# The first QKV stage of a conditioned transformer block: condition's rows first, the other small rows behind the modulation, filler transposes, weights in column slices

## The chip, the cores and the metric

The kernel runs on one core of a Trainium2 chip. The time is the device time of one execution in microseconds (us), and runs are compared by their medians. The engines are TensorE (PE; its weight loads are listed as PEld), VectorE (DVE), ScalarE (ACT), GpSimd (POOL) and SyncE (SP, which here only issues DMA transfers). Each engine works through its own instruction queue strictly in order; engines wait for each other and for transfers through semaphores.

## The reference

One transformer block whose two layer norms and two residual branches are modulated by a condition vector (batch 2, 2048 tokens, width 512, 16 heads, hidden width 2048):

```python
mod = silu(condition) @ Wada + bada
sh_a, sc_a, gt_a, sh_m, sc_m, gt_m = split(mod, 6, axis=1)
xn = layernorm(x, g1, be1)
xm = xn * (1.0 + sc_a[:, None, :]) + sh_a[:, None, :]
x = x + gt_a[:, None, :] * attention(xm, Wqkv, Wproj, bproj)   # causal
xn = layernorm(x, g2, be2)
xm = xn * (1.0 + sc_m[:, None, :]) + sh_m[:, None, :]
h = gelu(xm @ W1 + b1)
x = x + gt_m[:, None, :] * (h @ W2 + b2)
```

## The kernel before

The kernel goes through the two batch rows one after the other (a QKV stage, attention, projection each) and then through the MLP. The change lies in the first QKV stage, which also has to start everything: it loads the first tokens, the condition and the weights. In this stage 2048 tokens go by in groups of 512 (four tiles of 128 tokens), and for each group the queries, keys and values are made in blocks of 128 columns, most of them by a scheme with seven products in place of eight (`SUMS`: four extra weight blocks are sums and differences of the four that are loaded, `weight_sum`, on POOL). The very first block of queries and keys is made in the plain way (`plain`, tile `ps_qk`), so that it needs no sums.

What has to happen ahead of the first product:

- *Tokens.* `load_x(0)` (L919, SP) brings four tiles `x` of 256 KB. `stats` makes mean and variance (VectorE, L218 and L221); `inv_std` makes `rstd` (ScalarE Sqrt, L224; VectorE, L225 and L226); `scaled` applies them (ScalarE, L964, in place, one instruction for each tile). `norm(0, 0, ...)` transposes tiles 0 and 1 on TensorE (L214, tile `ps_xt`), `norm(0, 1, ...)` tiles 2 and 3.
- *Small rows.* The condition and the vectors g1, be1, g2, be2, b1, b2 are loaded as 44 rows of 128 numbers into one tile `rows` by seven DMAs that ScalarE issues (L1373). One transpose on TensorE (`ps_c`) and one copy on VectorE (L1402) turn them into columns, `cols`.
- *Modulation.* `load_wada(0, 1)` (L1391, SP) loads two 512 x 512 blocks of `Wada` in eight pieces of 256 KB into a free part of `vv`; POOL clears `mr` and loads `bada` into it. ScalarE makes `sc` = silu of the condition's columns (L1455). `modulation(0)` multiplies (tile `ps_mod`, eight products, shown as sixteen); `columns()` adds `bada` (VectorE, L1425), turns the result (`ps_modt`) and copies it to `mod`; `scale_shift` makes `a1` and `c1` out of it and of `cols`. `modulate` writes the modulated tokens `xmT` from the transposed ones (VectorE L269 and ScalarE L274).
- *Weights.* `load_w` (L926, SP) loads the four blocks of `Wqkv` for queries and keys, 512 KB each, `load_wv` (L936) the four for values. Behind them stand the sums on POOL (L944) and the tokens of the next group (L919 again).

ScalarE's functions come in tables. A function that is not in the loaded table needs an ACT_TABLE_LOAD ahead of it; the compiler puts it there. Silu and Sqrt lie in different tables. At L136 a tiny activation named `first` loads the Sqrt table early.

*What sets the order.* A scheduler of the framework orders each engine's instructions. What goes through `act()`, `mm()` or `transpose()` keeps the order in which it is written; the rest may move. Transfers that SP and ScalarE issue count their completions on eight semaphores, which are given out in turn over both queues, in the order in which the scheduler places the DMAs. A DMA that takes a semaphore first waits, on the engine that issues it, for the DMA that had the semaphore before it, which may be one of the other engine. In this kernel's built order the first eight are: `rows` (condition), x0, `rows` (g1), x1, `rows` (be1), `rows` (g2), x2, `rows` (be2). Then come x3, b1, b2, the eight pieces of Wada, `wqk` and `wv`.

The lines on which the waits of this case turn:

```python
def act(ins):
    return tc.keep_in_program_order(ins)

ps_c = ps_mm.tile([P, n_rows], F32, tag="mm", name="ps_c")
transpose(ps_c, rows)
nc.vector.tensor_copy(cols[:, :n_rows], ps_c)
```

Of the kernel before, what the change touches and what calls it, by code (L numbers as in the profile page):

```python
# [8 lines left out]
F32 = mybir.dt.float32  # L9
F32R = mybir.dt.float32r  # L10
BF16 = mybir.dt.bfloat16
AF = mybir.ActivationFunctionType
# [5 lines left out]
P = 128  # L18
# [9 lines left out]
def dit_block_kernel(  # L28
# [36 lines left out]
    nc = tc.nc  # L65
    B, T, D = x.shape
    HID = W1.shape[1]
    C = D // P
# [23 lines left out]
    ident = const.tile([P, P], F32, tag="ident", name="ident")  # L92
# [7 lines left out]
    eps = const.tile([P, 1], F32, tag="eps", name="eps")  # L100
# [16 lines left out]
    for n in range(2):  # L117

        f = bp.tile([P, QB + P], BF16, tag=f"fold{n}", name=f"fold{n}")
# [13 lines left out]


    first = const.tile([P, 1], F32, tag="first", name="first")
    nc.scalar.activation(first, eps, AF.Sqrt)  # L136


    cols = const.tile([P, 64], F32, tag="cols", name="cols")
# [15 lines left out]
    n_cond = B * C  # L155
    r_g1 = n_cond
    r_be1, r_g2, r_be2 = r_g1 + C, r_g1 + 2 * C, r_g1 + 3 * C
    r_b1 = r_g1 + 4 * C
    r_b2 = r_b1 + FC
    n_rows = r_b2 + C  # L160
# [36 lines left out]
    def col(r, n):  # L197
        return cols[:, r : r + n]
# [9 lines left out]
    def act(ins):  # L208

        return tc.keep_in_program_order(ins)  # L210

    def transpose(dst, src):
        n = src.shape[0]
        return tc.keep_in_program_order(nc.tensor.transpose(dst, src, ident[:n, :n]))  # L214
# [78 lines left out]
    ps_sp = ps_s_cm.__enter__()  # L293
# [590 lines left out]
    w_v = Wqkv.rearrange("(c p) f -> p c f", p=P)  # L884
# [11 lines left out]
    HK = C // 2  # L896

    class Qkv:
# [21 lines left out]
                xts.append(xt)  # L920
            self.xts[g] = xts

        def load_w(self, queue):
            for n, i, k in BASE:
                act(
                    queue.dma_start(  # L926
                        self.w[:, n], w_v[:, k * HK : (k + 1) * HK, i * D : (i + 1) * D]
                    )
                )

# [429 lines left out]
    with pool("wada") as wp, pool("qkv0") as qp, pool("hl0") as hp, pool(  # L1360
        "ps_qkv0", bufs=6, space=PSUM
    ) as ps_mm:
        rows = wp.tile([n_rows, P], F32, tag="rows", name="rows")
        for r, n, src in (
            (0, n_cond, cond.rearrange("b (c p) -> (b c) p", p=P)),
            (r_g1, C, g1.rearrange("(c p) -> c p", p=P)),
            (r_be1, C, be1.rearrange("(c p) -> c p", p=P)),
            (r_g2, C, g2.rearrange("(c p) -> c p", p=P)),
            (r_be2, C, be2.rearrange("(c p) -> c p", p=P)),
            (r_b1, FC, b1.rearrange("(c p) -> c p", p=P)),  # L1370
            (r_b2, C, b2.rearrange("(c p) -> c p", p=P)),
        ):
            nc.scalar.dma_start(rows[r : r + n, :], src)  # L1373
        wada_v = Wada.rearrange("(c p) f -> p c f", p=P)
        wada = {}

# [17 lines left out]
        qkv = Qkv(row, qp, ps_mm)  # L1394
        qkv.load_x(0)
        load_wada(0, 1)
        qkv.load_w(nc.sync)
        qkv.load_wv(hp, nc.sync)

        ps_c = ps_mm.tile([P, n_rows], F32, tag="mm", name="ps_c")  # L1400
        transpose(ps_c, rows)
        nc.vector.tensor_copy(cols[:, :n_rows], ps_c)  # L1402
        sc = wp.tile([P, C, HD], F32, tag="sc", name="sc")
        nc.vector.memset(sc, 0.0)

# [34 lines left out]
        def scale_shift(a, c, r_g, r_be, shift, scale):  # L1440
# [6 lines left out]
                )  # L1447
            nc.vector.tensor_tensor(c, c, mod[:, shift], ALU.add)

        for t in range(MTT):  # L1450
            qkv.stats(0, t)
        halves = [qkv.norm(0, 0, True)]

        act(
            nc.scalar.activation(  # L1455
                sc[:, :, :B], col(0, n_cond).rearrange("p (b c) -> p c b", c=C), AF.Silu
            )
        )
        picks()
        columns = modulation(0)  # L1460
        halves.append(qkv.norm(0, 1, True))
        columns()
        scale_shift(a1, c1, r_g1, r_be1, 0, 1)
        for k in range(0, C, 2):
# [62 lines left out]
    with pool("qkv1") as qp, pool("ps_qkv1", bufs=6, space=PSUM) as ps_mm:  # L1527
        qkv = Qkv(row, qp, ps_mm)
# [62 lines left out]
    with ExitStack() as mlp:  # L1591
        wp = mlp.enter_context(pool("mlpw", side="right"))
        ps_mm = mlp.enter_context(pool("ps2", bufs=4, space=PSUM))
# [733 lines left out]
```

## Time and profile before

| what | us |
| --- | --- |
| median of 3 runs | 2258.35 |
| the three runs | 2256.87, 2258.35, 2260.15 |
| the profiled execution | 2256.73 |
| its span, from the first to the last instruction | 2255.0 |
| mean granted TensorE clock, as a share of full speed | 0.997 |

A row of a timeline gives the start and the duration in us, the engine, the line of the kernel, the operation, output<-inputs by the program's names, their shapes, the count of instructions that were merged into the row, and in brackets how long the engine had been idle before and what ended that. ACTq and SPq are instructions that only issue a DMA. Rows of `ps_mod`, `ps_modt`, `ps_qk` and other float32 products show two entries for each product of the program. A row of a table of stretches gives for each engine its busy time and the count of instructions, and at its end the granted TensorE clock, the mean busy share of the sixteen DMA engines and the rate in GB/s.

### The profile page before, as it was taken

The page shows a single profiled execution, that of the slowest core. Times are in us where ns is not written, and L with a number is a line of the kernel's source. Part 1 is how long each engine was busy: PE and PEld are TensorE (multiplying, and loading weights), DVE is VectorE, ACT ScalarE, POOL GpSimd, SP SyncE. Part 2 cuts the span into 40 slices and gives each one's busy share as a digit, 9 for nine tenths or more (in the row PEclk, how much of TensorE's full clock was granted, in tenths as well). Part 3 has the DMA queues.
Part 4 walks back from the last instruction along what each step waited for, and adds up shares of the span by engine and source line. Part 5 has one row for each costly group of instructions (what it writes and reads, how often), then busy time and mean ns, then how long its engine had stood idle before and what let it go on. Part 6 is the DMA issues. An engine that isn't in the chain of part 4 may idle for free.

```text
span 2255.0 us, 33464 instructions
## 1 busy us (share of the span) xinstructions
PE 2211.3 (98%) x12057; PEld 1432.2 (64%) x12057; DVE 1535.7 (68%) x3309; ACT 1004.6 (45%) x2012; POOL 1297.9 (58%) x807
## 2 busy tenths in 40 slices
PE   7999999999999999999999999999999999999998
PEld 6777555555543587855555555345787787688687
DVE  4668766777757666777577767663685586576576
ACT  4434555555564244365656555614322422332410
POOL 4253998998983695199989898444205204304210
PEclk9999999999999999999999999999999999999999
DMA  8877143231324799542324113363353354353433
GB/s 281 251 259 193 43 93 75 62 85 48 106 97 135 252 308 313 142 92 62 85 67 104 44 48 131 109 231 129 109 175 133 123 184 145 108 187 126 158 125 110
DMA packets 160510, 311.57 MB, mean 138 GB/s; under 512 B 16544, under 2 KB 48844, under 8 KB 158552
## 3 DMA queue, kind: packets, MB, share of 16 engines
q1 hardware_dynamic: 155488, 285.53, 41.8%
q0 software_dynamic: 4480, 23.36, 2.7%
q8 instruction: 95, 1.56, 0.3%
q14 instruction: 71, 0.58, 0.1%
q10 hardware_dynamic: 376, 0.55, 0.1%
HBM read 229.95 MB, written 87.29 MB: 141 GB/s over the span
## 4 chain that ended last, share of the span: by engine, by line
PE 89%; DVE 4%; DMA 2%; POOL 2%; ACT 1%; issue 1%; SPq 0%; DVEq 0%; ACTq 0%; POOLq 0%
PE ps_a L206 27%; PE st L206 18%; PE ps_b L206 12%; PE o L206 10%; PE s L206 9%; PE ps_c L206 4%; PE ps_o L206 4%; PE sm L206 3%; DVE junk L498 1%; POOL ee L695 1%; PE ps_xt L214 1%; DMA x<-in_x_dram 1%; ACT e L670 1%; DVE mx L504 1%; PE ps_o L214 1%
## 5 line engine op out<-in xcount | busy, mean ns | idle before, releaser
L670 ACT ACTIVATE e<-st 128x512 f32<-128x512 f32 (+1 forms) x1152 | 575.0, 579 | 362.4 <-PE st L206 321.3
L504 DVE TENSOR_REDUCE mx<-s 128x1 f32<-128x512 f32 x576 | 381.9, 686 | 199.0 <-PE s L206 197.9
L695 POOL TENSOR_TENSOR ee<-ee,e 128x2048 f32<-128x2048 f32 x106 | 485.8, 4583 | 10.3 <-ACT e L670 4.3
L206 PE MATMUL st<-qst,kst 128*128 128x512 f32 (+3 forms) x1280 | 408.7, 386 | 0.0
L206 PE MATMUL s<-kst,qst 128*128 128x512 f32 (+3 forms) x1046 | 382.2, 396 | 8.0 <-DVE mx L498 2.7
L206 PE MATMUL ps_a<-sum,w 128*128 128x256 f32 (+1 forms) x1088 | 328.8, 431 | 0.1
L206 PE MATMUL o<-e,vv 128*32 128x512 f32 (+3 forms) x2560 | 293.2, 537 | 0.3 <-POOL e L682 0.3
L206 PEld LDWEIGHTS st<-qst,kst 128*128 128x128 f32 x1280 | 228.5, 188 | 97.3 <-issue 65.7
L498 DVE CUSTOM_DVE_ANT_0 junk<-s,causal 128x128 bf16<-128x128 f32 (+3 forms) x470 | 220.7, 470 | 61.0 <-PE s L206 46.8
L1795 POOL TENSOR_TENSOR sum<-w 128x256 f32<-128x256 f32 x30 | 21.8, 727 | 397.1 <-DMA w<-w1d 203.1
L206 PEld LDWEIGHTS s<-kst,qst 128*128 128x128 f32 x1046 | 195.4, 189 | 72.4 <-DVE mx L504 15.4
L206 PEld LDWEIGHTS ps_a<-sum,w 128*128 128x128 f32 x1088 | 204.5, 190 | 40.1 <-issue 11.4
L695 POOL TENSOR_TENSOR ee<-e 128x2048 f32<-128x2048 f32 x42 | 192.5, 4583 | 43.5 <-ACT e L670 42.5
L206 PEld LDWEIGHTS <-sel 32*128 32x128 bf16 x1152 | 29.5, 91 | 197.0 <-issue 196.1
L2014 ACT ACTIVATE h<-h,cols 128x512 f32<-128x512 f32 x120 | 76.8, 710 | 136.3 <-DVE h L1716 136.3
L504 DVE TENSOR_REDUCE mx<-st 128x1 f32<-128x512 f32 x192 | 131.0, 682 | 0.5
L682 POOL TENSOR_SCALAR_AFFINE_SELECT e<-e 128x512 f32<-128x512 f32 x128 | 83.3, 669 | 67.2 <-ACT e L670 67.2
L206 PE MATMUL st<-fold,sel 32*128 32x512 bf16 (+1 forms) x1152 | 117.3, 372 | 1.2
L206 PEld LDWEIGHTS o<-e,vv 128*32 128x32 f32 x2560 | 59.1, 108 | 92.3 <-issue 72.8
L1716 DVE TENSOR_TENSOR h<-c,ps_b 128x256 f32<-128x256 f32 x90 | 37.9, 421 | 103.5 <-PE ps_b L206 103.0
L1066 POOL TENSOR_TENSOR lo<-lo,hi 128x512 fp32r<-128x512 f32 x32 | 40.7, 1274 | 114.2 <-ACT hi L1064 109.8
L206 PE MATMUL ps_b<-sum,w 128*128 128x256 f32 (+1 forms) x384 | 95.0, 383 | 0.0
(237 smaller groups left out, 3590.7 us busy)
## 6 DMA issues: line engine op xcount, KB each, us to landing
qst<-q SPq DMA_DIRECT2D x128, 256.0 KB
kst<-k SPq DMA_DIRECT2D x128, 256.0 KB
w<-w1d SPq DMA_DIRECT2D x32, 896.0 KB
w<-w2d SPq DMA_DIRECT2D x28, 1024.0 KB
w<-w2d SPq DMA_DIRECT2D x28, 768.0 KB
q<-hi SPq DMA_DIRECT2D x32, 256.0 KB
q<-lo SPq DMA_DIRECT2D x32, 256.0 KB
k<-hi SPq DMA_DIRECT2D x32, 256.0 KB
```

The source lines that it names most:

```text
L206: return tc.keep_in_program_order(nc.tensor.matmul(*args, **kw))
L214: return tc.keep_in_program_order(nc.tensor.transpose(dst, src, ident[:n, :n]))
L498: nc.vector.tensor_tensor_reduce(junk[:, :w], x, causal[:, QB - w :], 1.0, MASKED, ALU.add, ALU.max, m,)
L504: self.vector(nc.vector.tensor_reduce(m, x, axis=AX.X, op=ALU.max))
L670: act(nc.scalar.activation(e4[:, h, :w], sts[h][:, :w], AF.Exp))
L682: nc.gpsimd.affine_select(d, d, pattern=[[0, HC], [1, P]], compare_op=ALU.is_ge, fill=0.0, base=0, channel_multiplier=-1,)
L695: act(nc.gpsimd.tensor_tensor(dst, x, y, ALU.add))
L1066: engine.tensor_tensor(lo, d, hi.bitcast(F32), ALU.subtract)
L1716: act(nc.vector.tensor_tensor(dst, x, y, ALU.add))
L1795: act(engine.tensor_tensor(dst, u, v, op))
L2014: nc.scalar.activation(d[j], d[j], AF.Gelu, bias=col(r_b1 + half * HF + fs[j], 1))
```

## The change

Six things change, all in the first QKV stage.

1. The condition's eight rows are loaded twice: first into a tile of their own, `rows_c`, then into `rows` as before. `rows_c` gets a transpose of its own, `ps_1`, and Silu reads that.
2. The small loads on ScalarE's queue go through `act()`, so their order is kept, and the Silu table is loaded by a tiny activation behind be1's load, ahead of the loads of g2, be2, b1 and b2.
3. Silu (`sc`) and a tiny Sqrt stand ahead of the statistics and the first `norm`; before, Sqrt was loaded first and Silu stood between the two halves of the tokens.
4. The transpose of `rows` and the copy to `cols` stand behind the second half's transposes, ahead of `columns()`.
5. TensorE makes 6 transposes of `ident` into a spare tile `ps_w` ahead of `ps_1` and 30 behind it.
6. The blocks of `Wqkv` for queries and keys are loaded in column slices: 128 columns of all four blocks, the next 128, then the last 256; twelve DMAs in place of four.

In the built order of the changed kernel the semaphores are given out to `rows_c`, x0, `rows` (condition), x1, g1, be1, x2, x3, then Wada 0 to 7, then g2, the first `wqk` piece, be2, the second piece, b1, the third, b2, the fourth, and the rest of `wqk`, `wv` and the next tokens. On POOL the memset of the next `mr`, which waits for `ps_modt`, and the two DMAs behind it stand among the weight sums instead of ahead of them.

```diff
--- before.py
+++ after.py
@@ -133,7 +133,6 @@
 
 
     first = const.tile([P, 1], F32, tag="first", name="first")
-    nc.scalar.activation(first, eps, AF.Sqrt)
 
 
     cols = const.tile([P, 64], F32, tag="cols", name="cols")
@@ -920,11 +919,12 @@
                 xts.append(xt)
             self.xts[g] = xts
 
-        def load_w(self, queue):
+        def load_w(self, queue, f=slice(0, D)):
             for n, i, k in BASE:
                 act(
                     queue.dma_start(
-                        self.w[:, n], w_v[:, k * HK : (k + 1) * HK, i * D : (i + 1) * D]
+                        self.w[:, n, :, f],
+                        w_v[:, k * HK : (k + 1) * HK, i * D + f.start : i * D + f.stop],
                     )
                 )
 
@@ -1361,6 +1361,7 @@
         "ps_qkv0", bufs=6, space=PSUM
     ) as ps_mm:
         rows = wp.tile([n_rows, P], F32, tag="rows", name="rows")
+        rows_c = wp.tile([n_cond, P], F32, tag="rowsc", name="rowsc")
         for r, n, src in (
             (0, n_cond, cond.rearrange("b (c p) -> (b c) p", p=P)),
             (r_g1, C, g1.rearrange("(c p) -> c p", p=P)),
@@ -1370,7 +1371,11 @@
             (r_b1, FC, b1.rearrange("(c p) -> c p", p=P)),
             (r_b2, C, b2.rearrange("(c p) -> c p", p=P)),
         ):
-            nc.scalar.dma_start(rows[r : r + n, :], src)
+            if not r:
+                act(nc.scalar.dma_start(rows_c, src))
+            act(nc.scalar.dma_start(rows[r : r + n, :], src))
+            if r == r_be1:
+                act(nc.scalar.activation(first, eps, AF.Silu))
         wada_v = Wada.rearrange("(c p) f -> p c f", p=P)
         wada = {}
 
@@ -1394,12 +1399,19 @@
         qkv = Qkv(row, qp, ps_mm)
         qkv.load_x(0)
         load_wada(0, 1)
-        qkv.load_w(nc.sync)
+        for f0, f1 in ((0, 1), (1, 2), (2, C)):
+            qkv.load_w(nc.sync, slice(f0 * P, f1 * P))
         qkv.load_wv(hp, nc.sync)
 
-        ps_c = ps_mm.tile([P, n_rows], F32, tag="mm", name="ps_c")
-        transpose(ps_c, rows)
-        nc.vector.tensor_copy(cols[:, :n_rows], ps_c)
+        ps_w = ps_sp.tile([P, P], F32, tag="s", name="ps_w")
+
+        def busy(n):
+            for _ in range(n):
+                transpose(ps_w, ident)
+
+        busy(6)
+        ps_1 = ps_sp.tile([P, n_cond], F32, tag="s", name="ps_1")
+        transpose(ps_1, rows_c)
         sc = wp.tile([P, C, HD], F32, tag="sc", name="sc")
         nc.vector.memset(sc, 0.0)
 
@@ -1447,18 +1459,23 @@
                 )
             nc.vector.tensor_tensor(c, c, mod[:, shift], ALU.add)
 
+        act(
+            nc.scalar.activation(
+                sc[:, :, :B], ps_1.rearrange("p (b c) -> p c b", c=C), AF.Silu
+            )
+        )
+        act(nc.scalar.activation(first, eps, AF.Sqrt))
+        busy(30)
         for t in range(MTT):
             qkv.stats(0, t)
         halves = [qkv.norm(0, 0, True)]
 
-        act(
-            nc.scalar.activation(
-                sc[:, :, :B], col(0, n_cond).rearrange("p (b c) -> p c b", c=C), AF.Silu
-            )
-        )
         picks()
         columns = modulation(0)
         halves.append(qkv.norm(0, 1, True))
+        ps_c = ps_mm.tile([P, n_rows], F32, tag="mm", name="ps_c")
+        transpose(ps_c, rows)
+        nc.vector.tensor_copy(cols[:, :n_rows], ps_c)
         columns()
         scale_shift(a1, c1, r_g1, r_be1, 0, 1)
         for k in range(0, C, 2):
```

## The prediction

> **What bounds the kernel now.** I read the page first, then the order of time on each engine over the first 30 us, because all of the change lies there.
>
> ```profile
> span 2255.0 us, 33464 instructions
> PE 2211.3 (98%) x12057; PEld 1432.2 (64%) x12057; DVE 1535.7 (68%) x3309; ACT 1004.6 (45%) x2012; POOL 1297.9 (58%) x807
> ```
>
> TensorE sets the end; whatever delays its first real product delays everything behind it. TensorE in order of time (start, duration, instruction, idle before and its releaser):
>
> ```profile
> 7.39 0.30 PE L214 MATMUL ps_c<-ident,rows 44*128 44x44 f32 x1 [7.39 <-DMA rows<-in_L_cond_b_dram]
> 9.19 0.48 PE L214 MATMUL ps_xt<-ident,x 128*128 128x128 f32 x1 [1.50 <-ACT x L964]
> 9.89 1.76 PE L214 MATMUL ps_xt<-ident,x 128*128 128x128 f32 x7 [0.23 <-ACT x L964]
> 11.58 2.75 PE L206 MATMUL ps_mod<-vv,sc 128*32 128x512 f32 x16
> 14.26 1.09 PE L214 MATMUL ps_xt<-ident,x 128*128 128x128 f32 x8
> 15.29 1.05 PE L206 MATMUL ps_modt<-pickc,mr 128*128 128x4 f32 x8
> 18.12 7.13 PE L206 MATMUL ps_qk<-xmT,wqk 128*128 128x512 f32 x16 [1.78 <-DVE xmT L269]
> ...
> 25.95 1.03 PE L206 MATMUL ps_b<-t,wqk 128*128 128x256 f32 x4
> 27.86 1.10 PE L206 MATMUL ps_a<-t,wqk 128*128 128x256 f32 x4 [0.89 <-POOL wqk L944]
> ```
>
> The first product is `ps_qk` at 18.12; from there TensorE hardly stops. Before it stands one chain: ScalarE scales the tokens `x`, TensorE transposes the first half, makes the modulation `ps_mod`, transposes the second half, and the modulated tokens `xmT` follow. ScalarE over the same stretch:
>
> ```profile
> 0.81 0.58 ACTq L1373 DMA_DIRECT2D rows<-in_cond_dram  x1
> ...
> 2.40 0.32 ACTq L1373 DMA_DIRECT2D rows<-in_L_cond_be_dram  x1
> 3.60 0.69 ACTq L1373 DMA_DIRECT2D rows<-in_L_cond_b_dram  x2
> ...
> 7.42 0.30 ACT L224 ACTIVATE rstd<-mv,eps 128x4 f32<-128x4 f32 x1 [1.61 <-DVE mv L221]
> 8.32 1.52 ACT L964 ACTIVATE x<-x,shift,rstd 128x512 f32<-128x512 f32 x2 [0.60 <-DVE shift L226]
> 9.86 1.28 ACT L1455 ACT_TABLE_LOAD   x1
> 11.15 0.21 ACT L1455 ACTIVATE sc<-cols 128x8 f32<-128x8 f32 x1
> ```
>
> The row to look at is 3.60. The fifth DMA issue ended at 2.72 and the sixth only began at 3.60. VectorE got its first tokens at the same moment:
>
> ```profile
> 3.60 0.69 DVE L218 BATCH_NORM_STATS2 stat<-x 128x6 f32<-128x512 f32 x1 [2.23 <-DMA x<-in_x_dram]
> ```
>
> So ScalarE's queue stood until a transfer of **another** queue had landed. The built program says why: SP's and ScalarE's DMAs share eight completion counters in rotation, and an issue waits on its own engine until the DMA eight places earlier has landed. Everything behind that issue waits too. SP shows the same: its `wv` issues go out as the Wada pieces land (us in total, times, longest).
>
> ```profile
> SPq L936 <- DMA vv<-in_L_cond_Wada_dram: 1.2, 4, 0.3
> ```
>
> **The change part by part.** *The counters.* The new order of issue is: `rows_c`, x0, `rows`, x1, g1, be1, x2, x3, Wada 0 to 7, and only then g2, be2, b1, b2, each beside a first `wqk` piece. As the changed kernel builds, g2 waits for Wada 0, be2 for Wada 2, b1 for Wada 4 and b2 for Wada 6, and on ScalarE's queue they stand **ahead** of the Silu of `sc`, the Sqrt table load, `rstd` and the scaling of all four token tiles, since `act()` keeps the written order. Before, `rstd` ran at 7.42 with nothing left before it but the statistics. Now nothing of this starts before Wada 6 has landed. Call that moment T.
>
> *T.* The `wv` issue that waited for Wada 6 shows when it landed:
>
> ```profile
> 12.18 0.37 SPq L936 DMA_DIRECT2D wv<-in_L_cond_Wqkv_dram  x1
> 12.87 0.68 SPq L936 DMA_DIRECT2D wv<-in_L_cond_Wqkv_dram  x1
> ```
>
> 12.18 for Wada 6, 12.87 for Wada 7. The transfers' rate by stretches (last columns: granted clock, DMA share, GB/s):
>
> ```profile
> 2.00:5.00 3.00, 0.00 (x0) 0.00 (x0) 1.36 (x3) 0.68 (x1) 3.00 (x8) 1.00 0.94 320
> 5.00:7.00 2.00, 0.00 (x0) 0.00 (x0) 1.56 (x5) 0.80 (x2) 0.41 (x1) 1.00 0.75 201
> 7.00:12.00 5.00, 2.89 (x13) 1.92 (x17) 1.22 (x10) 3.95 (x7) 0.00 (x0) 1.00 1.02 350
> 12.00:18.00 6.00, 4.34 (x32) 2.27 (x24) 2.21 (x8) 1.06 (x3) 1.30 (x3) 1.00 1.05 393
> ```
>
> There is a hole from 5 to 7 because Wada's issues waited for late rows. In the new rotation Wada waits for earlier transfers, so the hole should fill: (350 - 201) x 2 us = 298 KB, at 350 GB/s 0.85 us. I take T = 12.18 - 0.85 = 11.33. Bounds: 12.2 if the hole stays; 10.1 if the whole stretch ran at 393 ((393 - 320) x 3 + (393 - 201) x 2 + (393 - 350) x 5 = 818 KB, 2.1 us).
>
> *From T to the first product.* Issue of b2 0.32, Silu 0.21, table load 1.28, `first` 0.20 (as the 0.21 of the Silu), then `rstd` to the first scaling 0.90 (8.32 - 7.42): 2.9. From the first scaling to `ps_qk` the chain is the old one, 18.12 - 8.32 = 9.8; the transpose of the 44 rows that now stands before `ps_modt` (0.30) runs while VectorE makes `mr`, and the copy of `cols` fits under the 1.05 of `ps_modt`. First product at 11.33 + 2.9 + 9.8 = 24.0, against 18.12: **+5.9 us**.
>
> *TensorE kept busy.* The filler's transposes need only `ident`:
>
> ```profile
> 1.41 0.29 POOL masks.py:199 TENSOR_SCALAR_AFFINE_SELECT ident<-ident 128x128 f32<-128x128 f32 x1
> ```
>
> 36 of them from 1.7 on, at 0.25 each (1.76 / 7) or 0.14 (1.09 / 8), end between 6.6 and 10.7. The tokens come at about 15.1 (T + 2.9 + 0.8 for one scaling). That idle time, 4.4 us or more, undoes what the transposes were to buy, as another place shows:
>
> ```profile
> 876.68 0.33 PE L214 MATMUL ps_xt<-ident,x 128*128 128x128 f32 x1 [3.79 <-ACT x L964]
> 877.38 1.75 PE L214 MATMUL ps_xt<-ident,x 128*128 128x128 f32 x7 [0.38 <-ACT x L964]
> ...
> 876.00:880.00 4.00, 2.95 (x11) 2.57 (x12) 0.40 (x1) 3.71 (x7) 3.92 (x4) 0.61 0.95 203
> ```
>
> After 3.79 us idle seven transposes took 1.75 again, at a granted clock of 0.61. So I keep the old 9.8, which began slow too. The Trainium skill, "TensorE: Matmul & The Clock Gate", Part 1, says that the array falls to half its clock after about one idle window of 3.4 us and that this window runs free; by that rule too the filler buys nothing here, and the trace agrees with 3.79. Bounds: fast all along, 1.76 becomes 0.95 and `ps_mod` 1.72 (four times 7.13 / 16) instead of 2.68, -1.8; slow to the first product, `ps_mod` +0.7 and the sixteen small ones 0.11 each more, +2.5.
>
> *The table load moved.* Sqrt is loaded behind Silu, so the load that the next `rstd` needed falls away:
>
> ```profile
> 25.91 1.28 ACT L224 ACT_TABLE_LOAD   x1
> 27.20 0.30 ACT L224 ACTIVATE rstd<-mv,eps 128x4 f32<-128x4 f32 x1
> 27.40 0.36 ACT L1059 ACTIVATE lo<-ps_a 128x256 f32<-128x256 f32 x1
> ...
> 28.08 1.52 ACT L964 ACTIVATE x<-x,shift,rstd 128x512 f32<-128x512 f32 x2
> ```
>
> TensorE's stop before 27.86 is put down to POOL, but ends 0.1 after `lo<-ps_a` (27.40 + 0.36), which stood behind the load. The gain is small: `rstd` also needs the last statistics,
>
> ```profile
> 26.52 0.29 DVE L221 BATCH_NORM_AGGREGATE mv<-stat 128x2 f32<-128x6 f32 x2
> ```
>
> which end at 26.81, so `lo<-ps_a` gains some 0.4; and the built order puts one scaling (0.8) between it and `lo<-ps_b`, which the product behind needs. Bounds -0.6 and +0.8; I take 0. On the way from T to `rstd`, the Trainium skill, "ScalarE: Activation LUTs", What ACT_TABLE_LOAD costs, adds a drain of about 1.38 us to each load; here Silu ran at 11.15 straight after 9.86 + 1.28, so the trace does not bear it out. By the page the result would be an estimated 1.4 us later.
>
> *Weights by columns.* Eight pieces of 128 KB with rows of 512 bytes and four of 256 KB replace four of 512 KB; eight more issues stand on SP before `wv`. A like load:
>
> ```profile
> 89.80 2.95 SPq L1230 DMA_DIRECT2D kst<-in_L_cond_W_dram  x4
> ...
> 89.00:93.00 4.00, 4.00 (x25) 3.62 (x24) 0.81 (x3) 3.24 (x8) 0.00 (x0) 1.00 1.06 287
> ```
>
> At 287 instead of 393 GB/s the first 1.05 MB takes 3.7 instead of 2.7 us, +1.0 at most, nothing at least. From Wada 7 (12.87 - 0.85 = 12.0) on, `wqk` is in by 12.0 + 3.7 + 2.7 = 18.4; its first use is at 24.0. Hidden by the longer chain; without that cover it would be a rival, below. On POOL a memset that waits for `ps_modt` (then at 22) stands before five weight sums:
>
> ```profile
> 18.43 10.36 POOL L944 TENSOR_TENSOR wqk<-wqk 128x256 f32<-128x256 f32 x12 [0.18 <-DMA wqk<-in_L_cond_Wqkv_dram]
> ```
>
> 0.86 each, done by 28; they are columns that TensorE reaches after 31. Nothing.
>
> *Sum.* +5.9 on the profiled execution's 2256.73 us (span 2255.0 and 1.7 around it) is 2262.6. The runs' median, 2258.35, is 1.6 above that execution, so the forecast for a median is **2264.2**. Nothing later gives the time back: loads and sums of later stages are issued by TensorE's steps.
>
> **The rivals.** *The change does what it says.* If the wait for Wada 6 on ScalarE's queue is not there or ends early, the scaling stays at 8.32, the array is fast, and the transposes end at 9.84 + 0.95 = 10.8. `ps_mod` then ends with Wada 7: 12.0 + 0.43 = 12.4 instead of 14.26, the first product at 16.3, -1.8 us: **2256.5**. The first columns, 0.52 MB at 287 GB/s, are in by 13.9. The row at 3.60 and the built waits speak against it: 0.06.
>
> *The stall is there, but shorter:* an early T (10.1, -1.2) or a fast array (-1.8), one of them: +4.1 to +4.7, **2262.6**. The hole could close further; the idle time speaks against the fast array. 0.20.
>
> *The array stays slow to the first product* (+2.5): +8.4, **2266.7**. The old ramp, begun at 9.19, was over at 14.26, where eight transposes took 1.09, and by the same spacing it would be over before the second half's transposes now; a later end of it is less likely: 0.14.
>
> **How the numbers follow.** The forecast's own case, +4.8 to +7, has 0.60. About 0.2% (4.5 us) is what a measurement of this kernel can tell from no change. Slower by more than that: the forecast's case, the slow array, and a small part of the short stall, less a little for the runs' own spread of 3 us, 0.71. Within: most of the short stall and a part of the first rival, 0.24. Faster: 0.05. The range reaches from the short stall with both gains (+2.9 less a little) to the slow array with T at 12.2 and the runs' spread: 2260.3 to 2267.8.
>
> **What would show it.** Right: on ScalarE the issues of g2, be2, b1, b2 stand apart by some 1.4 us, the last near 11.3, Silu and a table load straight behind, `rstd` at 13 or later; TensorE idle from about 8 to 15, then transposes at 0.25 each; `ps_qk` near 24; no load before the second `rstd`. Wrong: `rstd` still near 7.5, or `ps_qk` before 18; or the same first product with the end moved by another amount, which would place the cause in a later stage.

## The result and the profile after

The changed kernel takes 2263.39 us (median of 13 runs, 2261.1 to 2267.64), the kernel before 2258.35 us (13 runs, 2253.94 to 2261.13): a ratio of 1.0029, 95% interval 1.0022 to 1.0037. It is slower by 0.29%, some 5 to 6.5 us. The profiled execution of the changed kernel took 2265.48 us, span 2263.8; that is 2.1 above its median, while the profiled execution of before lay 1.6 below its own. So the two spans differ by 8.8 us, more than the medians. Of these 8.8, some 1.5 lie behind the last computation, while the last results are stored: 4.96 us there against 3.50 in before; in the profile of e8, a kernel that is no slower than before, it is 5.34, so they are not counted as the change's.

ScalarE in order of time in the changed kernel (start, duration, instruction, idle time before and its releaser):

```profile
2.43 1.28 ACT L1378 ACT_TABLE_LOAD   x1 [2.43 <-issue]
...
7.31 0.25 ACTq L1376 DMA_DIRECT2D rows<-in_L_cond_g_dram  x1
8.72 0.25 ACTq L1376 DMA_DIRECT2D rows<-in_L_cond_be_dram  x1
10.30 1.60 ACTq L1376 DMA_DIRECT2D rows<-in_L_cond_b_dram  x2
12.01 0.18 ACT L1463 ACTIVATE sc<-ps 128x8 f32<-128x8 f32 x1 [8.08 <-DMA rows<-in_L_cond_b_dram]
12.20 1.28 ACT L1467 ACT_TABLE_LOAD   x1
...
13.61 0.28 ACT L223 ACTIVATE rstd<-mv,eps 128x4 f32<-128x4 f32 x1
14.33 2.93 ACT L964 ACTIVATE x<-x,shift,rstd 128x512 f32<-128x512 f32 x4 [0.44 <-DVE shift L225]
```

The four late issues stand at 7.31, 8.72, 10.30 and 11.64 (the row of 10.30 holds two; the second alone starts at 11.64), 1.3 to 1.6 apart, and ScalarE does nothing else from 3.93, where `first` ended, to 12.01. `rstd` is at 13.61 where it was at 7.42, the scaling at 14.33 where it was at 8.32: 6.0 us later.

TensorE in order of time:

```profile
3.43 4.32 PE L213 MATMUL ps_w<-ident 128*128 128x128 f32 x30
15.20 0.48 PE L213 MATMUL ps_xt<-ident,x 128*128 128x128 f32 x1 [7.45 <-ACT x L964]
15.90 1.76 PE L213 MATMUL ps_xt<-ident,x 128*128 128x128 f32 x7 [0.23 <-ACT x L964]
17.59 2.51 PE L205 MATMUL ps_mod<-vv,sc 128*32 128x512 f32 x16
...
25.08 8.83 PE L205 MATMUL ps_qk<-xmT,wqk 128*128 128x512 f32 x16 [2.79 <-DVE xmT L268]
...
36.98 1.10 PE L205 MATMUL ps_b<-xmT,wqk 128*128 128x256 f32 x4 [0.47 <-ACT lo L1059]
```

The first product starts at 25.08 instead of 18.12, 6.96 later, after 2.79 us of idle time (1.78 before), and its sixteen matmuls take 8.83 instead of 7.13. The stretches of half clock show why (last columns: granted clock, DMA share, GB/s):

```profile
11.99:18.82 6.83, 3.40 (x16) 1.94 (x20) 0.34 (x2) 4.78 (x8) 1.99 (x3) 0.50 0.77 219
18.82:25.65 6.83, 4.04 (x31) 2.38 (x23) 4.12 (x10) 0.99 (x3) 4.60 (x8) 1.00 1.02 354
25.65:29.06 3.41, 3.41 (x6) 1.36 (x5) 3.41 (x7) 0.95 (x3) 3.40 (x6) 0.50 0.67 246
```

The clock was halved at 11.99, in the long idle time, came back at 18.82, and was halved again at 25.65, just behind the first product's start: 3.41 us at half clock cost 1.70. The extra idle time ahead of that product is VectorE's. Its operations there, and GpSimd's weight sums beside them:

```profile
22.62 0.69 DVE L1455 SCALAR_TENSOR_TENSOR c<-mod,cols 128x8 f32<-128x8 f32 x1
23.34 0.65 DVE L1460 TENSOR_TENSOR c<-c,mod 128x8 f32<-128x8 f32 x1
24.03 1.90 DVE L268 TENSOR_SCALAR xmT<-ps_xt,a,c 128x256 f32<-128x256 f32 x4
```

```profile
16.83 2.91 POOL L944 TENSOR_TENSOR wqk<-wqk 128x256 f32<-128x256 f32 x4 [11.41 <-DMA wqk<-in_L_cond_Wqkv_dram]
21.88 2.09 POOL L944 TENSOR_TENSOR wqk<-wqk 128x256 f32<-128x256 f32 x3 [2.15 <-DMA wqk<-in_L_cond_Wqkv_dram]
```

The two small operations on `c`, eight columns each, took 0.69 and 0.65 us while three weight sums of 0.70 (2.09 / 3) ran back to back. In the kernel before there were no weight sums yet, and the same two took 0.16 and 0.17:

```profile
16.67 0.16 DVE L1443 SCALAR_TENSOR_TENSOR c<-mod,cols 128x8 f32<-128x8 f32 x1
16.87 0.17 DVE L1448 TENSOR_TENSOR c<-c,mod 128x8 f32<-128x8 f32 x1
```

Followed along the run, the same product starts this much later in the changed kernel: 6.96 at the first, 8.25 from the first half-stage to 70 us (6.96 + 1.70 of clock - 0.42, because the stop of 0.89 behind the first `ps_b` became one of 0.47), 9.44 at 90 to 118, only 4.93 at 126, some 5 until 860, 7.6 at 890 and 7.3 at the end. What happens at 120 stands in the queue of SyncE, TensorE's order of time and the clock. SyncE's issues of W in before, then in the changed kernel:

```profile
107.57 4.91 SPq L1230 DMA_DIRECT2D kst<-in_L_cond_W_dram  x4
```

```profile
117.01 1.97 SPq L1230 DMA_DIRECT2D kst<-in_L_cond_W_dram  x4
```

TensorE's stop in the attention steps, again before first:

```profile
119.86 0.80 PE L206 MATMUL s<-kst,qst 128*128 128x512 f32 x1 [2.75 <-DVE mx L498]
```

```profile
127.04 0.50 PE L205 MATMUL s<-kst,qst 128*128 128x512 f32 x1 [0.48 <-DVE mx L497]
```

And before's clock there:

```profile
119.11:125.94 6.83, 6.08 (x14) 4.88 (x15) 5.19 (x15) 0.82 (x2) 2.31 (x3) 0.50 0.59 203
```

In before the four issues took 4.91 us, the tokens behind them came late, TensorE stopped for 2.75 and fell to half clock for 6.83. In the changed kernel the issues took 1.97 and the stop was 0.48. Near 880 us TensorE stands for 3.79 in before and for 4.52 in the changed kernel, and the half-clock stretch there lasts 3.41 and 6.83: that is most of the step from some 5 to 7.6.

### The profile page after: what moved, and what is told of

Read it like the earlier page. It is cut to its first block, busy times and chain, and to the rows that moved or that the text cites. A ratio compares the mean times of both kernels' runs of the same rounds, so it can differ in the third digit from the quotient of the medians.

```text
span 2263.8 us, 33551 instructions
## 1 busy us (share of the span) xinstructions
PE 2218.3 (98%) x12094; PEld 1436.2 (63%) x12094; DVE 1534.0 (68%) x3309; ACT 1003.3 (44%) x2012; POOL 1297.9 (57%) x807
## 4 chain that ended last, share of the span: by engine, by line
PE 87%; DVE 3%; POOL 2%; DMA 1%; ACT 1%; issue 1%; SPq 0%; DVEq 0%; ACTq 0%; POOLq 0%
PE ps_a L205 25%; PE st L205 18%; PE ps_b L205 11%; PE o L205 10%; PE s L205 9%; PE ps_o L205 4%; PE ps_c L205 4%; PE sm L205 3%; POOL ee L694 1%; DVE junk L497 1%; PE ps_xt L213 1%; ACT e L669 1%; DVE mx L503 1%; PE ps_o L213 1%; DMA x<-in_x_dram 0%
```

## The experiments

The theory was the prediction's: the late rows' issues, waiting on ScalarE's queue for pieces of Wada, make the whole loss. The rivals were that another part of the change makes it (columns, filler, table loads), or that the shift of the first stage is given back whatever its size. Each median below has its ratio to the kernel before, with the 95% interval; both ran on the same chip. A difference between two such ratios takes it that a ratio is the same on every chip: e1 to e4, e5 to e8 and e9 to e11 ran on three different ones. An edit also lets the scheduler order GpSimd's queue anew, so a run can differ from its partner by more than the lines shown; where this matters it is said.

### e1: late rows issued on GpSimd

```
-            act(nc.scalar.dma_start(rows[r : r + n, :], src))
+            queue = nc.gpsimd if r > r_be1 else nc.scalar
+            act(queue.dma_start(rows[r : r + n, :], src))
```

> The changed kernel with one edit: the loads of g2, be2, b1 and b2 are issued on GpSimd's queue, not on ScalarE's. Everything else of the change stays. Theory (these four issues wait for Wada 0, 2, 4 and 6 on ScalarE's own queue, and rstd and the scaling wait behind them): ScalarE has no issue behind be1 to stand at, rstd is back near 7.5 us and the first scaling near 8.3 (14.33 in the changed kernel), the first product ps_qk starts at 16.3 to 17.5 (25.08 in the changed kernel, 18.12 before), and the time is 1 to 2 us below the kernel before, some 6.5 us below the changed kernel. Rival (the columns, the filler or the order of the table loads cost the time): the time stays 4 to 6 us above the kernel before, whatever ScalarE's queue does. Second rival (the first stage's shift is given back later anyway): the first product moves by 7 us and the end by less than 3.

2261.52 us, 1.0016 (1.0007 to 1.0024). The wait is gone: `rstd` at 8.48, scaling at 9.27, first product at 18.95, 6.1 us earlier than in the changed kernel, though not at the 16.3 to 17.5 expected. Yet the time fell by only 0.13% +/- 0.11%, some 3 us, and is still above before. TensorE of e1:

```profile
10.84 0.98 PE L213 MATMUL ps_xt<-ident,x 128*128 128x128 f32 x7 [0.38 <-ACT x L964]
...
18.95 10.20 PE L205 MATMUL ps_qk<-xmT,wqk 128*128 128x512 f32 x16 [2.80 <-DVE xmT L268]
...
33.16 1.10 PE L205 MATMUL ps_a<-t,wqk 128*128 128x256 f32 x4 [2.28 <-POOL wv L949]
```

The filler now does what it is for (0.98 for seven transposes, not 1.76), but two losses take the place of the wait: `ps_qk` takes 10.20 under a half-clock stretch of 6.83, and 2.28 us of stop stand ahead of `ps_a`. Both lead to VectorE, shown first, and to GpSimd's weight sums beside it:

```profile
16.49 0.70 DVE L1456 SCALAR_TENSOR_TENSOR c<-mod,cols 128x8 f32<-128x8 f32 x1
17.22 0.65 DVE L1461 TENSOR_TENSOR c<-c,mod 128x8 f32<-128x8 f32 x1
...
20.51 6.07 DVE L997 TENSOR_TENSOR t<-xmT,t 128x512 f32<-128x512 f32 x2
```

```profile
20.65 2.09 POOL L944 TENSOR_TENSOR wqk<-wqk 128x256 f32<-128x256 f32 x3
22.69 0.54 POOL L1391 DMA_DIRECT2D mr<-in_L_cond_bada_dram  x1
23.24 3.91 POOL L944 TENSOR_TENSOR wqk<-wqk 128x256 f32<-128x256 f32 x5
```

Two sums of tokens, 2.16 us together before, took 6.07. The first ended only after a run of three weight sums had ended (22.74), the second after a run of four. VectorE's statistics stand behind them, ScalarE's `rstd` behind the statistics, and `lo<-ps_a`, which frees the bank that TensorE wants, behind `rstd`: 32.49 + 0.30 for `rstd`, 32.70 + 0.37 for the copy, TensorE at 33.16. The releaser that the row names, `wv`, is not the one that ended the stop.

So the theory holds for what delays the first product and falls as the whole account of the time. The number of the second rival, an end that moves by less than 3 us, came about; not by a give-back later in the run, but by these two losses.

### e2: the columns alone, in the kernel before

```
...
-        qkv.load_w(nc.sync)
+        for f0, f1 in ((0, 1), (1, 2), (2, C)):
+            qkv.load_w(nc.sync, slice(f0 * P, f1 * P))
```

> The kernel before with one part of the change alone: the first stage's weights wqk are loaded by columns, 12 pieces for 4. Theory (the slices cost nothing and bring nothing by themselves): ps_qk still starts within 0.5 us of 18.12, the time is within 1 us of the kernel before; at most +1.0, the time that 1.05 MB takes longer at 287 than at 393 GB/s, shows in the landing of the last wqk piece. Rival (the slices are what the change costs: eight more issues on SP and short rows delay wqk and wv): the first product or the products just behind it stall, and the time is 3 us or more above the kernel before.

2258.19 us, 1.0005 (0.9996 to 1.0014): nothing to be measured, as forecast. First product at 17.73. `ps_qk` took 8.83 after the same 1.78 of idle time with which before had 7.13: the clock again, a half-clock stretch of 3.41 at 18.96. Here too the built order has four weight sums ahead of the memset of `mr`. The first began at 16.59, when VectorE's second small operation had begun at 16.48, so that the two still took 0.16 and 0.17.

### e3 and e4: without the filler

```
-        busy(6)
...
-        busy(30)
```

e3 is the changed kernel without these two lines, e4 is e1 without them.

> The changed kernel without the 36 filler transposes. Theory (TensorE idles 7.45 us between the filler and the first transposes of tokens, and this idle time undoes the filler): the eight transposes behind the scaling still take 1.7 to 1.8 us for seven, the first product starts within 0.3 us of 25.08, and the time is within 1 us of the changed kernel. Rival (the filler brings part of its gain in spite of the idle time): transposes and ps_mod take longer without it, first product 0.5 to 2 us later and the time with it. Second rival (the filler harms, by delaying the first transpose or ps_1 or by what it draws): the first product comes earlier than 25.08.

> The changed kernel with g2, be2, b1 and b2 issued on GpSimd's queue and without the 36 filler transposes. Beside the run with the filler it gives what the filler is worth once TensorE need not idle. Theory: with the filler the last of its transposes ends near 7.8 us and tokens come near 9, so TensorE is at full clock for the first half's transposes (0.95 us for seven, 1.76 without) and for ps_mod (1.72 where Wada doesn't hold it, 2.7 without): without the filler the first product is 0.5 to 1.8 us later than with it, and the time 0.5 to 1.8 us longer. Rival (ps_mod ends with Wada's last piece, whatever the clock): the two first products are within 0.3 us of each other.

e3: 2268.89 us, 1.0053 (1.0040 to 1.0066), against 1.0029 for the changed kernel. The theory said no difference; it is 0.24%, +/- 0.15% by the two intervals. The seven transposes took 1.76 in both, as the theory had it, but `ps_mod` took 3.64 (2.51 with the filler), and the first product started at 26.55. e4: 2263.68 us, 1.0029 (1.0018 to 1.0041), against 1.0016 of e1: in the expected direction, 0.13% +/- 0.14%, so not separated from nothing; first product 19.28 against 18.95. The 0.24% are not the filler's alone: without it GpSimd's built order is another, with twelve weight sums ahead of the memset of `mr` where the changed kernel has seven. In e3 VectorE's second sum of tokens began at 28.69, ran beside three sums of `wv` and took 4.50 (0.67 in the changed kernel); the second `rstd` stood at 39.38 instead of 34.74, and TensorE stopped for 1.90 ahead of `ps_a`. How much of the difference the filler itself makes stays open; the place of the clock's windows differs between the two profiles as well.

### e5 and e6: whole weights again

```
-        for f0, f1 in ((0, 1), (1, 2), (2, C)):
-            qkv.load_w(nc.sync, slice(f0 * P, f1 * P))
+        qkv.load_w(nc.sync)
```

e5 is e1 with this edit, e6 the changed kernel with it.

> The kernel of e1 (late rows issued on GpSimd) with the weights wqk in four whole pieces, as before the change. In e1 GpSimd's weight sums began at 16.44 us, while VectorE made the modulation's columns, whose two small operations then took 0.70 and 0.65 us (0.16 and 0.17 before); TensorE idled 2.80 us and ran ps_qk for 10.20 us under a half-clock stretch of 6.83 us. Theory A (the columns cost this, by letting the sums start before the columns of the modulation are made): with whole pieces the sums start after 18 us, the small operations are back at 0.17, the idle time ahead of ps_qk is 1.7 to 1.9, ps_qk starts below 17.9 and takes 7 to 9 us; time 1.5 to 4 us below e1, so -1 to +1.5 against the kernel before. Rival B (the half clock is a matter of where TensorE's slack falls, whatever GpSimd does): small operations back at 0.17, but a half-clock stretch of 3.4 to 6.8 us all the same, time within 1 us of e1 (+2.5 to +4).

> The changed kernel with the weights wqk in four whole pieces: only the column slices are undone, the late rows stay on ScalarE's queue. Theory A (columns let GpSimd's sums collide with VectorE's small operations): two operations of 0.17 instead of 0.69 and 0.65, first product 24.0 to 24.3 (25.08 in the changed kernel), time 1 to 3 us below the changed kernel, so +2 to +4 against the kernel before. Prediction's own step (the slices cost and bring nothing): time within 0.7 us of the changed kernel, +4.3 to +5.7. Rival (the whole pieces come too late for the first product): they land at 18.4 or later, far ahead of 24, so no stall is expected; if the first product or ps_a waits for wqk, this rival holds.

e5: 2264.45 us, 1.0028 (1.0018 to 1.0039); e6: 2269.04 us, 1.0047 (1.0034 to 1.0061). Both are above their partners with columns (1.0016 and 1.0029), where theory A and the prediction's own step expected them below or equal. In e5 theory A came true at the place that it spoke of, the small operations at 0.16 and 0.17, 1.78 us idle, first product at 17.64. Rival B came true as well, `ps_qk` taking 8.69 with a half-clock stretch of 3.41 at 17.39, and the loss moved on. TensorE of e5:

```profile
27.03 1.03 PE L205 MATMUL ps_b<-t,wqk 128*128 128x256 f32 x4
33.04 2.04 PE L205 MATMUL ps_a<-t,wqk 128*128 128x256 f32 x4 [4.99 <-POOL wv L949]
```

VectorE and then ScalarE of e5, ahead of that stop:

```profile
22.22 2.65 DVE L997 TENSOR_TENSOR t<-xmT,t 128x512 f32<-128x512 f32 x1
24.80 3.08 DVE L1489 COPY pick<-pickc 128x512 f32<-128x512 f32 x1
```

```profile
32.37 0.30 ACT L223 ACTIVATE rstd<-mv,eps 128x4 f32<-128x4 f32 x1 [5.41 <-DVE mv L220]
32.58 0.36 ACT L1059 ACTIVATE lo<-ps_a 128x256 f32<-128x256 f32 x1
```

A sum and a copy of 0.7 to 0.9 us took 2.65 and 3.08 beside the weight sums, so `rstd` came at 32.37 and TensorE stood for 4.99. That VectorE is held up where GpSimd's runs of sums meet it is the cause that fits all of these.

In e6 theory A fails at its first step. GpSimd and then VectorE of e6:

```profile
19.11 4.95 POOL L944 TENSOR_TENSOR wqk<-wqk 128x256 f32<-128x256 f32 x7 [13.70 <-DMA wqk<-in_L_cond_Wqkv_dram]
```

```profile
22.83 0.58 DVE L1459 TENSOR_TENSOR c<-c,mod 128x8 f32<-128x8 f32 x1
```

With whole weights, too, the built order has seven sums ahead of the memset of `mr`, and beside a chain that is late anyway they still meet it: VectorE's operations on `a` and `c` took 0.57, 0.15 and 0.58, TensorE idled 2.58, and `ps_qk` started at 24.49 and took 9.58 under a stretch of 6.83 at half clock. VectorE's sums of tokens are not the loss there (0.67 for the second and the third). So in the changed kernel it is not the columns that make sums and chain collide, but the late chain and the order in which GpSimd's work was built.

### e7: filler across the gap ahead of the first product

```
         columns()
+        ps_w = ps_sp.tile([P, P], F32, tag="s", name="ps_w")
+        for _ in range(18):
+            transpose(ps_w, ident)
```

> The kernel of e1 with 18 more filler transposes between ps_modt and ps_qk, where TensorE idled 2.80 us in e1. They fill 2.5 us at full clock. Theory C (the half clock of e1's ps_qk comes from TensorE's slack between 14 and 19 us): no half-clock stretch begins at 18 to 19, ps_qk takes 6.9 to 7.3 us instead of 10.20, the products behind it start 3 us earlier; time 2 to 3.5 us below e1, so about +0 to +1.5 against the kernel before. Rival D (the half clock comes whatever stands there, or the loss is made up at the later stop behind ps_b): ps_qk shorter, but ps_a waits the longer, the time within 1 us of e1; or ps_qk still 10 us.

2260.64 us, 1.0010 (1.0002 to 1.0019). TensorE of e7:

```profile
18.39 7.13 PE L205 MATMUL ps_qk<-xmT,wqk 128*128 128x512 f32 x16 [0.25 <-DVE xmT L268]
...
31.59 2.05 PE L205 MATMUL ps_a<-t,wqk 128*128 128x256 f32 x4 [4.34 <-POOL wv L949]
```

Theory C holds for `ps_qk`: 7.13, at full clock. Rival D holds for the time: the end of `ps_b` came 3.6 us earlier than in e1 and the stop behind it grew from 2.28 to 4.34, long enough for a half-clock stretch of its own. Against e1 0.06% is left, inside the intervals.

### e8 and e9: GpSimd's sums held back

```
+        hold = wp.tile([P, 1], F32, tag="hold", name="hold")
+        act(nc.gpsimd.tensor_copy(hold, qkv.xmT[0][:, C - 1, :1]))
         for f in (1, 2, 3):
             for k in range(4):
                 qkv.weight_sum(nc.gpsimd, k, slice(f * P, (f + 1) * P))
```

e8 is e1 with this edit, e9 the changed kernel with it.

> The kernel of e1 with GpSimd's weight sums held back until VectorE has written the last modulated column of the first half: one copy of a column on GpSimd stands ahead of them and reads it. Theory A (the collision of GpSimd's sums with VectorE's small operations lengthens the chain): the small operations take 0.17 each, ps_qk starts 1.0 us earlier than 18.95, after 1.7 to 1.9 us idle; sums start near 18.5 as before the change; time 1 to 3 us below e1. Rival (VectorE's 6 us in the sums of tokens t and the stop of 2.28 us behind ps_b are the larger part, and come from GpSimd's sums lying later): first product earlier, but the stop ahead of the second ps_a as long or longer, time within 1 us of e1.

> The changed kernel with GpSimd's weight sums held back as in e8, the late rows still on ScalarE's queue: the missing corner beside the changed kernel (wait, no hold), e1 (no wait, no hold) and e8 (no wait, hold). Additive theory: the wait on ScalarE costs its 6 to 7 us in the first product whatever GpSimd does, the hold gives back 1 us there (idle time ahead of ps_qk 1.78 instead of 2.79, small operations 0.17), first product 24.0 to 24.2; time 4 to 6 us above the kernel before less 1, so +3 to +5, and 6 to 7 above e8. Rival (GpSimd's sums on VectorE are the main loss, the late start is hidden by what waits for weights and sums behind it): time within 1.5 us of e8, -1 to +1 against the kernel before. Third possibility: with the hold the sums end later than TensorE needs them, and a stop behind ps_b appears; then no gain on the changed kernel.

e8: 2257.19 us, 0.9996 (0.9986 to 1.0005); e9: 2262.15 us, 1.0022 (1.0012 to 1.0033). TensorE of e8, then GpSimd:

```profile
17.11 8.53 PE L205 MATMUL ps_qk<-xmT,wqk 128*128 128x512 f32 x16 [1.78 <-DVE xmT L268]
...
28.09 1.10 PE L205 MATMUL ps_a<-t,wqk 128*128 128x256 f32 x4 [0.72 <-POOL wqk L944]
29.91 1.10 PE L205 MATMUL ps_b<-xmT,wqk 128*128 128x256 f32 x4 [0.72 <-POOL wv L949]
```

```profile
18.57 10.01 POOL L944 TENSOR_TENSOR wqk<-wqk 128x256 f32<-128x256 f32 x12
```

The hold put the two issues of `mr` ahead of the sums, so that twelve sums run as one, at 0.83 each; VectorE's two small operations took 0.16 and 0.17 and its two sums of tokens 2.31. Theory A holds in its rows. Against e1 it is 0.20% +/- 0.13%, some 4.5 us, more than the 1 to 3 expected, as the stop ahead of `ps_a` shrank too, from 2.28 to 0.72, where the rival had it as long or longer. As a table of ratios:

| | late rows on ScalarE | late rows on GpSimd |
|---|---|---|
| sums not held | 1.0029 (changed kernel) | 1.0016 (e1) |
| sums held | 1.0022 (e9) | 0.9996 (e8) |

From the upper left to the lower right it is 0.33% +/- 0.12%, 7.5 us (the two intervals put together as squares, as in the other differences): the whole loss. The wait alone is worth 0.13% +/- 0.11% with the sums free and 0.26% +/- 0.14% with them held. The hold alone is worth 0.20% +/- 0.13% without the wait, but only 0.07% +/- 0.13% with it, which is not separated from nothing. In e9 the first product started at 24.96, where 24.0 to 24.2 had been expected: the idle time ahead of it fell to 1.78 as forecast, but `ps_mod` was slower (3.32 for 2.51), `ps_qk` took 10.00 under a half-clock stretch of 6.83, and a stop of 1.42 stands ahead of the next `ps_b` (0.47 in the changed kernel), as the third possibility had it, though that stop ends with ScalarE's `lo<-ps_b` (38.48 + 0.36). The table is additive to within the intervals; the rival that GpSimd's sums are the main loss is out, e9 being 0.26% above e8.

### e10 and e11: attempts at a faster kernel

e10 is e8 with the late rows issued behind the first ones of bada on GpSimd, and 12 transposes of filler ahead of `ps_qk`; e11 is e10 with the sums held until VectorE's three sums of tokens are done.

The lines with `range(12)` are e10's, the moved loads left out; the other two are what e11 changes in e10.

```
+        for _ in range(12):
+            transpose(ps_w, ident)
...
-        act(nc.gpsimd.tensor_copy(hold, qkv.xmT[0][:, C - 1, :1]))
+        act(nc.gpsimd.tensor_copy(hold, qkv.operands(0)[A22][:, HK - 1, :1]))
```

> The kernel of e8 with 12 filler transposes ahead of ps_qk (1.7 us at full clock, for 1.78 of idle time in e8), and with the late rows issued on GpSimd behind the rows of bada. If a half-clock stretch comes from slack in a window whose place changes from run to run, no stretch begins between 12 and 25 us, ps_qk takes 6.9 to 7.2 us, starts at 16.6 to 17.4, and the time is 1 to 2 us below e8 (-1.5 to -3 against the kernel before). Rival (what TensorE gains is lost again at the stop behind ps_b, where ScalarE's rstd waits for VectorE's statistics): the stop grows from 0.72 twice to 2.5 us or more and the time is within 0.7 us of e8.

> The kernel of e10 with GpSimd's weight sums held back further, until VectorE has made its three sums of tokens t. If VectorE's sums beside GpSimd's are what makes the statistics, rstd and the copies of ps_a late, VectorE's three sums take 0.7 us each, rstd comes 1.5 us or more earlier than in e10, and the stops behind ps_b go; time 0.5 to 2 us below e10. Rival (the weight sums are then late themselves): products of the second column of weights wait for GpSimd between 31 and 36 us, and the time is above e10's.

e10: 2258.10 us, 1.0005 (0.9996 to 1.0013); e11: 2257.60 us, 1.0004 (0.9993 to 1.0014). Neither beats before or e8. TensorE of e10, then ScalarE:

```profile
17.21 7.13 PE L205 MATMUL ps_qk<-xmT,wqk 128*128 128x512 f32 x16 [0.41 <-DVE xmT L268]
...
28.20 1.10 PE L205 MATMUL ps_a<-t,wqk 128*128 128x256 f32 x4 [2.13 <-POOL wqk L944]
```

```profile
27.54 0.30 ACT L223 ACTIVATE rstd<-mv,eps 128x4 f32<-128x4 f32 x1 [2.55 <-DVE mv L220]
27.74 0.36 ACT L1059 ACTIVATE lo<-ps_a 128x256 f32<-128x256 f32 x1
```

`ps_qk` starts 0.91 earlier than before, at full clock, and TensorE then stands for 2.13, because `rstd` is at 27.54 where before had it at 27.20. A half-clock stretch of 3.41 follows at 29.85. The rival of e10's expectation holds: the next group's statistics set the pace behind the first product, and what is won ahead of it is lost there. In e11 VectorE's last two sums of tokens took 1.42 together, 0.71 each, as expected, and `rstd` still came at 27.92: the statistics waited 2.22 for their tokens instead.

### e12: the kernel before once more

> The kernel before, once more, for its trace. In its first profile ps_qk ran at full clock (7.13 us) after 1.78 us of idle time, and a half-clock stretch of 6.83 us lay at 119.11. If the place of the windows in which TensorE's clock is set is free from run to run, then this profile may have ps_qk at 7.1 or at about 8.8 us (as the run of the columns alone had, with the same idle time), and any stretches start at other times, those of one run a multiple of 3.41 us apart. If the clock follows the program alone: 7.13 again, and the stretch at 119 again.

2256.61 us. Besides that of the last rows there is one half-clock stretch:

```profile
874.87:881.69 6.82, 5.13 (x16) 4.20 (x17) 1.97 (x4) 5.10 (x9) 6.74 (x8) 0.50 0.96 202
```

It lies in the stage where the first profile had 3.41 us at 876.87. As expected of windows, its distance from the one in the last rows, 2253.85, is 404 times 3.413. There is none at 119, though the stop was there again, 2.12 behind issues of W that took 4.90:

```profile
109.92 4.90 SPq L1230 DMA_DIRECT2D kst<-in_L_cond_W_dram  x4
121.59 0.50 PE L206 MATMUL s<-kst,qst 128*128 128x512 f32 x1 [2.12 <-DVE mx L498]
```

`ps_qk` took 7.13 again, but `ps_mod` 4.18 (2.75 in the first profile), and the first product started at 18.99. The stop of some 2.5 us at 120 thus came in both profiles of this kernel, the half clock behind it in one.

## Why the prediction was right in its number, and where its steps failed

The forecast, 2264.2 (2260.3 to 2267.8), holds the measured 2263.39, and its main step is shown. Some terms that were put at nothing were not, and partly made up for each other; that the number came so close is in part luck.

| step | forecast | measured |
|---|---|---|
| T, the landing of Wada 6 on which b2 waits | 11.33 | 11.64 |
| from T to the first scaling | 2.9 | 2.7 (11.64 to 14.33) |
| from the scaling to `ps_qk` | 9.8 | 10.75 |
| first product against before | +5.9 | +6.96 |
| `ps_qk` itself | 0 | +1.70 |
| table load, the stop behind `ps_b` | 0 (-0.6 to +0.8) | -0.42 |
| later stages, to the last product | 0 | -0.9 in the profile: +1.2 near 85, -4.5 at 120 (2.3 of it the stop, the rest before's half clock), +2.6 near 880, -0.3 behind |

- **The counters.** Right. The issues stand 1.3 to 1.6 us apart behind Wada's pieces, Silu, table load and `rstd` straight behind them. Taken off ScalarE's queue (e1, e8) the scaling is back at or below 9.3. The hole in the transfers closed (340 GB/s from 5 to 7 us instead of 201): T is 0.5 earlier than before's 12.18, not 0.85. The reason given for the hole is only in small part what the record shows: in before SyncE's issues of Wada waited 1.2 us in all for tokens and 0.2 for late rows.
- **"From the first scaling to `ps_qk` the chain is the old one, 9.8."** This step failed, by 0.95. The prediction saw that GpSimd's sums would move (its memset "stands before five weight sums ... Nothing") and asked only when TensorE needs the columns. It did not ask what runs beside them: in the new built order seven sums start ahead of that memset, and three of them ran beside VectorE's two small operations on the chain. That holds with whole weights too (e6). The hold of e8 and e9 takes it away: 0.16 and 0.17.
- **The clock.** The idle time did undo the filler for the transposes (1.76). The rival of a slow array had the right sign but the wrong place: the clock was back before `ps_mod` was through, and fell a second time, behind a gap of 2.79 us, into `ps_qk`. The Trainium skill, "TensorE: Matmul & The Clock Gate", Part 1, says that the windows are 3.4 us long and free-running, not tied to the kernel's start. The stretches here agree: 3.41 or 6.83 long, and in the two profiles of before at different places. So behind a short gap a stretch in one profile is a matter of chance, and only the gap that makes it possible belongs to the program; e7 and e10, with the gap filled, had none there. Behind a long gap it is not: near 880 us TensorE stands for 3.29 to 4.60 in all fourteen profiles, and each has a stretch there, of 3.41 or 6.83. A slip in the working of this step is small: four times 7.13 / 16 is 1.78 and not 1.72.
- **The filler at nothing.** Not borne out: without it the kernel is 0.24% slower (e3). That run's order on GpSimd is another as well, so what the filler itself is worth stays open.
- **Columns at nothing.** Right alone (e2). Inside the change the comparison goes against the step: without them the kernels are 0.12% and 0.18% slower (e5, e6); the first is within its +/- 0.14% of zero, the second just outside its +/- 0.15%.
- **The table load.** The load ahead of the second `rstd` is gone, and the stop behind it shrank within the bounds given. On the way to `rstd` the load of 1.28 was followed at once by `first` (12.20 to 13.50), so the drain that was weighed there doesn't show.
- **"Nothing later gives the time back."** Not borne out as a zero: 2.75 us of stop at 120 became 0.48 (2.12 in the second profile of before). But it is not the late start that is given back. e8, whose first product is at 17.11, has the same: its issues of W there took 2.43, and TensorE stops there for 0.23 at most. Why these issues on SyncE take 1.97 or 2.43 instead of 4.90 wasn't tried.
- **The rival "the change does what it says", 2256.5.** e8 and e10 are nearly that kernel: no wait, full clock ahead of the modulation, first product at 17.1 to 17.2 and not 16.3. They give 2257.2 and 2258.1, no measurable gain: `rstd` of the next group then holds TensorE, and each profile has a half-clock stretch of 3.41 close by (at 16.55 in e8, at 29.85 in e10).

## What to carry to other kernels

A DMA issue that may wait stands in line with an engine's own work: put late loads on a queue whose engine has nothing urgent behind them, and follow what each wait holds up. When a change reorders an engine's queue, or lets a load come earlier, ask also which work now goes ahead and what that work runs beside. And before paying for an earlier first product, look some ten microseconds on: here the next group's statistics, `rstd` and a bank's copy set the pace, and what e10 had won ahead of them was lost at that stop.

## What the runs showed of the hardware

VectorE beside GpSimd. An eight-column operation took 0.57 to 0.72 instead of 0.16 while weight sums of 0.72 ran; a sum of tokens took up to 3.2 us in e1, 4.50 in e3, instead of 0.7. The four steps that make `xmT` out of `ps_xt`, which lies in PSUM, took 1.90 in the changed kernel and in e1 beside weight sums (from 24.40; from 16.44 to 19.33), as they did in e8, where no sum ran beside them. The Trainium skill, "SBUF — State Buffer", Who interferes with whom, says that a VectorE instruction with two SBUF inputs contends with a GpSimd instruction that reads SBUF, that the shared ports are an exclusive lock, and that the order of issue decides who blocks. The first figure agrees, at most one sum waited for. The second does not fit that order: in e1 a sum of tokens began at 20.51, ahead of the weight sum at 20.65, and was held through three of them, the next through four. Where twelve sums ran as one group, in before and in e8, the two engines took turns (1.03 to 1.17 us for each of VectorE's, 1.06 to 1.17 for those of GpSimd's beside them, where alone they take 0.72). What makes the one or the other stays open.

TensorE's clock fell on gaps as short as 1.78 us behind the small matmuls of `ps_modt` (e2, e5 and e8: 3.41 us at half clock; e9: 6.83), and did not fall on the same 1.78 us in the two profiles of before.
